# The last norms of a fused eight-block network on one core: from channel-major sums by matmul to token-major statistics

## The chip, the core and the metric

The kernel runs on one core of one Trainium2 chip. A core has five engines that run their own instruction queues beside each other and wait for one another by semaphores: TensorE (PE, matmuls and transposes), VectorE (DVE), ScalarE (ACT), GpSimd (POOL) and SyncE (SP, which here issues DMAs). Matmuls write PSUM; everything else lives in SBUF, 128 partitions wide. The metric is device time of one launch in microseconds.

## The reference

A batch of 8 sequences of 256 tokens with 128 channels (2048 tokens) passes through eight blocks, each followed by a residual addition and a layer norm over the channels, without gain and offset:

```
x = layernorm(x + rglru(x));        x = layernorm(x + local_attention(x))
x = layernorm(x + mamba(x));        x = layernorm(x + experts1(x))
x = layernorm(x + chunked_attention(x)); x = layernorm(x + experts2(x))
x = layernorm(x + typed_attention(x));   x = layernorm(x + ternary_linear(x))

def layernorm(x): m, v = mean(x), var(x);  return (x - m) / sqrt(v + 1e-5)

experts2:  shared = silu(x @ sg) * (x @ su) @ sd          # 1024 hidden channels, every token
           routed = sum over a token's 2 chosen experts of gate * expert(x)   # 8 experts, capacity 320
           result = shared + routed
typed_attention: 16 heads of 8 channels, causal, half of the heads with a decay;
           softmax(q k^T / sqrt(8) + bias) v, then @ w_o
ternary_linear:  x @ w_eff + bias
```

The change concerns the last four lines of work: the sum and the norm behind experts2, and the two norms and the linear layer behind typed attention. What feeds them is the norm behind chunked attention.

## The kernel before, in words

The kernel is written stage by stage (`rglru`, `local_mamba`, `moe1`, `chunked`, `moe2`, `typed`), and each stage mixes several pieces of work by Python generators: a `yield` in a piece is where the mixer may go on with another one. The order in which the Python code issues instructions is, for each engine, close to the order in which it runs them.

**Layouts.** Activations between the stages are held by channel: a tile of 128 partitions (channels) by 2048 columns (tokens), `y` or `self.x`. By token means 128 tokens on the partitions and 128 channels in the row; a sequence then is two such halves, `[128, 2, 128]`.

**Two ways to norm.** `layernorm_steps` (L426) works by channel. The mean over the partitions is a matmul with a constant matrix (`ln_mean`), then DVE subtracts, ACT squares, a second matmul sums the squares (`ln_var`), ACT computes the inverse root as `Exp(-0.5 * Ln(v + eps))`, and DVE multiplies. All of it runs over 128x256 per sequence. `normed` (L1240), used in the chunked stage, works by token: `bn_stats` and `bn_aggr` on DVE give mean and variance of each row, ACT computes the inverse root for 128x2 numbers, and one DVE `tensor_scalar` per half subtracts and scales. `by_channel` (L1256) then transposes the result on PE.

**The end of `chunked`** (L1399). Each sequence's normed rows `z` are transposed into `y`, and `route2` makes the routing from them.

**`moe2`** (L1470). The common expert runs in four pieces of 512 tokens, `shared(i)` (L1486): 8 steps of two matmuls (`pg`, `pu`), a Silu on ACT, a product `sh` on DVE, and one matmul that adds to `acc` (128 channels by 512 tokens). Piece 0 comes ahead of the routed experts, piece 1 behind the issue of the gathers, pieces 2 and 3 after that. `got` (L1542) holds, for each of 16 token groups, two gathered rows per token, fetched by POOL's indirect DMA. `results(b)` (L1544) multiplies them by the gates, adds them, transposes the sum (`back`), adds the common expert's piece, norms by `layernorm_steps` and leaves the result in `y`. `results(0)` and the projections of sequence 0 are advanced one step after each step of pieces 2 and 3. ACT's function table has to be changed between Silu and Ln/Exp; `exp_ln` (L414) asks for the second, and `self.norm` and `self.silu` keep some of these in order.

**`typed`** (L1722). A sequence is six units: two of the first 128 queries (8 heads each) and four of the second (4 heads each, 256 keys). The loop over units is a pipeline of four: for unit i it issues the transposes `pt` of unit i-3, the scores `sc` of unit i, the softmax of unit i-1 and the outputs `o` of unit i-3. The softmax is: the row maximum `nm` on DVE (L1681), eight or four exponentials with row sums on ACT (L1686), the reciprocal `rc` on DVE (L1688), and the product `e * rc` on POOL (L1689, 128x1024). Between these, one to three steps of `side` work are issued: `results(b+2)`, the projections `before(b+2)`, and `after(b)` (L1726), which is the output projection `wo` with its residual and norm, the ternary layer `lin` with its bias, residual and norm, and the DMA out. So the order on each engine is set by this loop: a step of `side` stands behind the softmax instructions of the unit that was issued ahead of it. All matmuls, whichever piece calls them, are recorded at L394, and transposes of `pt` at L475.

Of the kernel before, what the change touches and what calls it, by code (L numbers as in the profile page):

```python
# [12 lines left out]
F32 = mybir.dt.float32  # L13
BF = mybir.dt.bfloat16
I32 = mybir.dt.int32
AF = mybir.ActivationFunctionType
ALU = mybir.AluOpType
# [4 lines left out]
P = 128  # L22
B = 8
S = 256
T = B * S
NT = T // P
EPS = 1e-5
# [127 lines left out]
def _layout(d):  # L155

    d = {k: np.asarray(v) for k, v in d.items()}
    f = np.float32
    out = {}
# [59 lines left out]
    for l in range(2):  # L219
        w = d["L0_ffn_wqkv"][l]  # L220
        q, k, v = w[:, :512], w[:, 512:1024], w[:, 1024:]
# [15 lines left out]
    rows = np.zeros((96, 4, P), f)  # L237
    rows[::32] = np.stack([d["L2_attn_" + n] for n in ("la_pb", "lf_b2", "sa_pb", "pf_b2")])
    out["b2"] = rows.reshape(96, 4 * P)
    out["w2"], out["wf"] = np.concatenate(lay, 1), np.concatenate(ffn, 1)  # L240
    for n in ("rg", "ru", "rd", "sg", "su", "sd"):
        out["e2" + n] = d["L2_ffn_" + n]
# [54 lines left out]
class _Kernel:  # L297
# [128 lines left out]
    def layernorm_steps(self, pool, src, dst, eps=EPS, tag="ln", steps=False):  # L426

        nc = self.nc
        n = src.shape[-1]
        if not steps and n <= S:  # L430

            ps = self.psum(name="ln")
            xc, var = ps[:, 0:n], ps[:, S : S + n]
            self.mm(xc, self.centre, src)
            sq = pool.tile([P, n], F32, tag=tag + "sq", name="ln_sq", bufs=2)
            nc.scalar.activation(sq, xc, AF.Square)
            self.mm(var, self.mean, sq)
            rs = pool.tile([P, n], F32, tag=tag + "rs", name="ln_rs", bufs=2)
            nc.scalar.activation(rs, var, AF.Ln, bias=eps)
            nc.scalar.activation(rs, rs, AF.Exp, scale=-0.5)  # L440
            nc.vector.tensor_mul(dst, xc, rs)
            return
        mean = self.psum(name="ln_mean")[:, :n]
        self.mm(mean, self.mean, src)
        xc = pool.tile([P, n], F32, tag=tag + "xc", name="ln_xc")
        nc.vector.tensor_sub(xc, src, mean)
        sq = pool.tile([P, n], F32, tag=tag + "sq", name="ln_sq")
        nc.scalar.activation(sq, xc, AF.Square)
        yield
        var = self.psum(name="ln_var")[:, :n]  # L450
        self.mm(var, self.mean, sq)
        rs = pool.tile([P, n], F32, tag=tag + "rs", name="ln_rs")
        nc.scalar.activation(rs, var, AF.Ln, bias=eps)
        self.norm = nc.scalar.activation(rs, rs, AF.Exp, scale=-0.5)
        yield
        nc.vector.tensor_mul(dst, xc, rs)  # L456

    def softmax(self, small, work, sc, groups, keys, tag):

# [888 lines left out]
    def chunked(self):  # L1348
        nc, tc = self.nc, self.tc
        w = self.wf  # L1350
        y = self.y_next
# [4 lines left out]
        with (  # L1356
# [42 lines left out]
            def one_sequence(b):  # L1399
# [33 lines left out]
                nc.any.tensor_copy(y[:, cs], self.by_channel(z))  # L1433
                yield 0.3, 0.8
                self.logits(b, y, self.w1[:, 866:874], self.lg2[:, 2 * b : 2 * b + 2, :])
                assert self.routed == b
                self.routed = b + 1
                self.rest = self.route2(b, z, work, small)
# [5 lines left out]
                    next(self.rest)  # L1444

            self.routed = 0
            on_pe([one_sequence(b) for b in range(B)], 3, [self.typed_weights(prep)])
        self.chunk_scope.close()
        self.x = y
# [20 lines left out]
    def moe2(self):  # L1470
# [9 lines left out]
        with (  # L1480
# [5 lines left out]
            def shared(i):  # L1486
                cs = bass.ts(i, 512)
                acc = self.psum("S", "acc")
                for c in range(8):
                    pg, pu = self.psum("A", "pg"), self.psum("A", "pu")  # L1490
                    self.mm(pg, gu[:, 0, c * P : (c + 1) * P], x[:, cs])
                    self.mm(pu, gu[:, 1, c * P : (c + 1) * P], x[:, cs])
                    h = work.tile([P, 512], F32, tag="sh", name="sh")
                    i = nc.scalar.activation(h, pg, AF.Silu)
                    if self.norm:

                        self.issue_after([i], self.norm)
                        self.norm = None
                    self.silu = i
                    self.paced = nc.vector.tensor_mul(h, h, pu)  # L1500
                    self.mm(acc, down[:, c * P : (c + 1) * P], h, c == 0, c == 7)
                    yield
                s = keep.tile([P, 512], F32, name=f"s{i}")
                nc.vector.tensor_add(s, acc, x[:, cs])
                ss.append(s)


            self.norm = None
# [34 lines left out]

            def results(b, work):  # L1544

                ps = self.psum("M", "back")
                for j in range(2):
                    t = 2 * b + j
                    r1, r2 = got[t]

                    i = nc.vector.tensor_scalar(r1, r1, self.gate2[:, 0, t : t + 1], None, ALU.mult)
                    self.issue_after([i], self.paced)
                    nc.vector.scalar_tensor_tensor(r1, r2, self.gate2[:, 1, t : t + 1], r1, ALU.mult, ALU.add)  # L1553
                    nc.tensor.transpose(ps[:, j * P : (j + 1) * P], r1, self.ident)
                s = work.tile([P, S], F32, tag="s", name="s")
                nc.vector.tensor_add(s, ss[b // 2][:, b % 2 * S : (b % 2 + 1) * S], ps[:, 0:S])
                yield
                if b == 0:
                    self.exp_ln(self.silu)
                yield from self.layernorm_steps(work, s, y[:, bass.ts(b, S)], steps=True)  # L1560

            self.results = results
            for _ in shared(1):
                pass
            self.x = y
# [145 lines left out]
    def typed_start(self):  # L1711
        one, self.ty, self.tys = self.pool("ty1"), self.pool("ty", 2), self.pool("tys", 6)
        self.vms, self.inputs = [], {}
        for i in range(2):
            vm = one.tile([P, 2, 8 * 136], F32, name=f"vm{i}")
            self.nc.gpsimd.memset(vm, 0.0)
            self.vms.append(vm)

    def typed_before(self, b):
        self.inputs[b] = yield from self.typed_inputs(self.x[:, bass.ts(b, S)], self.vms[b % 2], self.ty)  # L1720

    def typed(self):  # L1722
# [3 lines left out]
        def after(b, o):  # L1726
            cs = bass.ts(b, S)
            ot = work.tile([P, S], F32, tag="ot", name="ot")
            nc.scalar.copy(ot, o)
            yield  # L1730
            ps = self.psum("M", "wo")
            self.mm(ps[:, 0:S], self.w3[:, 640:768], ot)
            s = work.tile([P, S], F32, tag="s", name="s")
            nc.vector.tensor_add(s, ps[:, 0:S], self.x[:, cs])
            yield
            yield from self.layernorm_steps(work, s, s, steps=True)
            ps = self.psum("M", "lin")
            self.mm(ps[:, 0:S], we, s)
            s2 = work.tile([P, S], F32, tag="s2", name="s2")
            nc.vector.scalar_tensor_tensor(s2, ps[:, 0:S], self.v("bias"), s, ALU.add, ALU.add)  # L1740
            yield
            yield from self.layernorm_steps(work, s2, s2, steps=True)
            nc.sync.dma_start(self.out[:, cs], s2)

        units = [(b, u) for b in range(B) for u in [(0, 0, 4), (0, 4, 8)] + [(1, r, r + 2) for r in range(0, 8, 2)]]
        n = len(units)
# [70 lines left out]
```

## Time and profile before

| | |
|---|---|
| runs | 1905.53, 1902.89, 1902.8 us; median 1902.89 |
| the profiled execution's own time | 1898.62 us |
| its span | 1896.8 us |
| granted TensorE clock, mean | 0.91 |
| PE / DVE / ACT / POOL busy | 84% / 58% / 54% / 30% |
| moe2 after the gathers to the end | 1578 to 1897 us |
| steady state of typed | about 1680 to 1840 us, one sequence each 31.7 us |

In the profile a line gives engine, source line, operation, the tile written and read with their shapes, and a time; `x2` counts instructions that were put together. The line of stretches gives, from left to right, the window and its length, busy time of PE, PE's weight loads, DVE, ACT and POOL with their counts, the granted clock (1.00 is full), the busy share of the DMA engines and GB/s. In the timeline, brackets at the end of a line hold the idle time of that engine ahead of the instruction and what ended it.

### The profile page before, as it was taken

The numbers are of one execution on the slowest core, as the hardware profiler recorded it, in microseconds if no ns is written. First come the engines' busy times: TensorE is split into PE (matmuls) and PEld (weight loads), VectorE is DVE, ScalarE is ACT, GpSimd is POOL, SyncE is SP. The second block draws the span as 40 slices with busy tenths as digits, with TensorE's granted clock in tenths as the row PEclk, the third lists the DMA queues.
The fourth block names the chain that finished last, engine by engine and source line by source line (L and its number), as shares of the span: only waits on it lengthen the run. The fifth ranks groups of instructions, "written<-read, shape, count | busy, mean of one in ns | idle before, by whom it ended". The sixth has DMA issues, their size and how long they took to land. (4 is left out here: it accounts for less than half of the span.)

```text
span 1896.8 us, 28424 instructions
## 1 busy us (share of the span) xinstructions
PE 1585.0 (84%) x10810; PEld 957.3 (50%) x10810; DVE 1093.2 (58%) x2011; ACT 1020.7 (54%) x2702; POOL 560.4 (30%) x493
## 2 busy tenths in 40 slices
PE   3678887878788778786679999999988987899997
PEld 2344554535454444343656566665554733455554
DVE  5734458687779686679234554456443222467664
ACT  4557777667767877554234455444433312365654
POOL 1324443344342423203120211111111042255452
PEclk7789998989899988888789999999998997899998
DMA  4000002111112122366300000000101310000000
GB/s 172 1 1 1 1 35 56 35 56 35 45 46 56 35 56 68 95 215 167 102 24 2 10 6 6 6 5 5 36 2 29 104 39 13 1 4 4 7 4 9
DMA packets 58328, 75.50 MB, mean 40 GB/s; under 512 B 5868, under 2 KB 35236, under 8 KB 57168
## 3 DMA queue, kind: packets, MB, share of 16 engines
q1 hardware_dynamic: 52864, 67.57, 12.2%
q0 software_dynamic: 3216, 5.07, 0.9%
q8 instruction: 85, 1.39, 0.3%
q10 hardware_dynamic: 2112, 1.05, 0.2%
q14 instruction: 51, 0.42, 0.1%
HBM read 65.46 MB, written 9.71 MB: 40 GB/s over the span
## 5 line engine op out<-in xcount | busy, mean ns | idle before, releaser
L394 PE MATMUL y<-hs,ident 128*128 128x512 f32 x256 | 152.7, 727 | 38.0 <-DVE hs L794 37.8
L793 DVE TENSOR_TENSOR_SCAN hs<-da,hs 128x1024 f32<-128x1024 f32 x64 | 153.5, 2404 | 1.8 <-ACT da L789 1.6
L475 PE MATMUL pt<-ident,e 128*128 128x128 f32 x768 | 125.6, 291 | 23.7 <-POOL e L652 12.4
L652 POOL TENSOR_TENSOR e<-e,rc 128x1024 f32<-128x1024 f32 x32 | 67.9, 2121 | 232.6 <-DVE rc L651 232.6
L1686 ACT ACTIVATE e<-sc,nm 128x128 f32<-128x128 f32 (+1 forms) x256 | 104.1, 424 | 59.8 <-DVE nm L1681 57.5
L789 ACT ACTIVATE da<-d,na 128x255 f32<-128x255 f32 x256 | 111.8, 503 | 37.6 <-DVE hs L793 18.8
L1689 POOL TENSOR_TENSOR e<-e,rc 128x1024 f32<-128x1024 f32 x48 | 91.9, 1915 | 135.7 <-DVE rc L1688 102.4
L647 ACT ACTIVATE e<-sc,nm,rn 128x128 f32<-128x128 f32 x256 | 113.4, 462 | 24.9 <-DVE nm L642 22.4
L475 PEld LDWEIGHTS pt<-ident,e 128*128 128x128 f32 x768 | 90.2, 147 | 64.1 <-issue 22.4
L1298 POOL TENSOR_TENSOR e<-e,rc 128x512 f32<-128x512 f32 x32 | 33.5, 1048 | 295.7 <-DVE rc L1297 178.9
L599 POOL TENSOR_TENSOR t<-t,t 128x512 f32<-128x512 f32 x64 | 90.9, 1421 | 95.4 <-DVE t L586 79.0
L477 ACT COPY ptsb<-pt 128x512 f32<-128x512 f32 x94 | 55.1, 587 | 96.3 <-PE pt L475 87.5
L791 DVE TENSOR_TENSOR hs<-u,bc 128x1024 f32<-128x1024 f32 x64 | 86.2, 1357 | 34.0 <-POOL u L778 29.4
L394 PEld LDWEIGHTS y<-hs,ident 128*128 128x128 f32 x256 | 53.8, 226 | 97.6 <-DVE hs L794 51.7
L1273 ACT COPY kp<-kps 128x512 f32<-128x512 f32 x128 | 74.8, 584 | 41.7 <-PE kps L394 39.8
L1122 POOL DMA_INDIRECT got<-ybuf,get x48 | 45.5, 949 | 162.2 <-DMA ybuf<-ys 116.7
L477 DVE COPY ptsb<-pt 128x512 f32<-128x512 f32 x98 | 65.6, 685 | 33.5 <-PE pt L475 33.3
L394 PE MATMUL qk<-w_local,h 128*128 128x512 f32 x128 | 71.5, 648 | 14.1 <-DVE t L586 9.7
L794 DVE TENSOR_TENSOR hs<-hs,bc 128x1024 f32<-128x1024 f32 x64 | 80.0, 1256 | 0.2
L1246 DVE BATCH_NORM_STATS2 st<-out 128x6 f32<-128x128 f32 x80 | 20.0, 288 | 93.8 <-PE out L394 86.8
L1681 DVE TENSOR_REDUCE nm<-sc 128x4 f32<-128x1024 f32 (+1 forms) x48 | 58.6, 1220 | 24.6 <-PE sc L394 24.3
L1309 ACT COPY vs<-vps 128x512 f32<-128x512 f32 x64 | 37.4, 584 | 65.6 <-PE vps L394 44.1
(394 smaller groups left out, 3899.9 us busy)
## 6 DMA issues: line engine op xcount, KB each, us to landing
bc<-xs SPq DMA_DIRECT2D x128, 256.0 KB
w_attn<-in_w_dram SPq DMA_DIRECT2D x4, 1024.0 KB
w_local<-in_w_dram SPq DMA_DIRECT2D x2, 1557.0 KB
places<-zeros SPq DMA_DIRECT2D x2, 1280.0 KB
w_moe<-in_e1gate_dram SPq DMA_DIRECT2D x8, 256.0 KB
w_moe<-in_e1up_dram SPq DMA_DIRECT2D x8, 256.0 KB
w_moe<-in_e1down_dram SPq DMA_DIRECT2D x8, 256.0 KB
w_moe<-in_e2rg_dram SPq DMA_DIRECT2D x8, 256.0 KB
```

Source lines behind the costliest of these rows:

```text
L394: return self.nc.tensor.matmul(out, lhsT, rhs, start=start, stop=stop)
L475: self.last = self.nc.tensor.transpose(pt[:, j * P : (j + 1) * P], src[:, j * P : (j + 1) * P], self.ident)
L477: self.nc.any.tensor_copy(sb.rearrange("p a b -> p (a b)"), pt)
L599: nc.gpsimd.tensor_add(t1, t1, t2)
L647: nc.scalar.activation(e[:, j, g, :], scs[:, j, g, :], AF.Exp, bias=nm[:, j, g : g + 1], scale=rq[:, j, g : g + 1], accum_out=sm[:, j, g : ...
L789: nc.scalar.activation(da[:, n, c, 1:S], d[:, c, 1:S], AF.Exp, scale=na[:, i : i + 1])
L791: nc.vector.tensor_tensor(hs, u.unsqueeze(1).to_broadcast(shp), bn, ALU.mult)
L793: nc.vector.tensor_tensor_scan(line(hs), line(da), line(hs), 0.0, ALU.mult, ALU.add)
L794: nc.vector.tensor_tensor(hs, hs, cn, ALU.mult)
L1273: nc.scalar.copy(k[:, 2 * i : 2 * i + 2, :].rearrange("p a b -> p (a b)"), ps)
L1686: nc.scalar.activation(e[:, i, :], sc[:, i, :], AF.Exp, bias=nm[:, i : i + 1], accum_out=sm[:, i : i + 1])
L1689: nc.gpsimd.tensor_tensor(e, e, rc.unsqueeze(2).to_broadcast([P, n, keys]), ALU.mult)
```

## The change

After it, the sums and norms behind experts2 and typed attention are by token.

- `chunked` also stores each sequence's rows `z` in a DRAM buffer, by token (128 KB on SP's queue).
- `shared(i)` loads 512 tokens of these rows into `s{i}` (256 KB) and computes `acc` by token: four matmuls of 128 columns with the hidden tile stationary in the place of one of 512. The sum goes into the loaded tile.
- `results(b)` adds the four gated rows straight into that tile with `scalar_tensor_tensor`, norms with the new `token_norm`, and transposes the normed rows into `y` with the new `channels`. The tile is kept, as `self.rows(b)`.
- `after(b)` computes `wo` and `lin` by token (two matmuls of 128 columns each, activations stationary), takes the residual from `self.rows(b)`, norms with `token_norm`, transposes once for `lin` and once for the output, and adds the bias on POOL, from a tile `bias3` in which `typed_start` loads the bias row into all partitions. The copy out of PSUM is on ACT in both places, and the DMA out takes that copy.

The diff, without the bias row's place in the inputs:

```diff
@@ -454,6 +455,28 @@
         self.norm = nc.scalar.activation(rs, rs, AF.Exp, scale=-0.5)
         yield
         nc.vector.tensor_mul(dst, xc, rs)
+
+    def token_norm(self, src, dst, small):
+
+        nc = self.nc
+        st = small.tile([P, 2, 6], F32, tag="st", name="st")
+        mv = small.tile([P, 2, 2], F32, tag="mv", name="mv")
+        for t in range(2):
+            nc.vector.bn_stats(st[:, t, :], src[:, t, :])
+            nc.vector.bn_aggr(mv[:, t, :], st[:, t, :])
+        rs = small.tile([P, 2], F32, tag="rs", name="rs")
+        nc.scalar.activation(rs, mv[:, :, 1], AF.Ln, bias=EPS)
+        self.norm = nc.scalar.activation(rs, rs, AF.Exp, scale=-0.5)
+        yield
+        for t in range(2):
+            nc.vector.tensor_scalar(dst[:, t, :], src[:, t, :], mv[:, t, 0:1], rs[:, t : t + 1], ALU.subtract, ALU.mult)
+
+    def channels(self, z, dst, copy):
+
+        ps = self.psum("M", "zt")
+        for t in range(2):
+            self.nc.tensor.transpose(ps[:, t * P : (t + 1) * P], z[:, t, :], self.ident)
+        copy(dst, ps[:, 0:S])
 
     def softmax(self, small, work, sc, groups, keys, tag):
 
@@ -1433,6 +1456,7 @@
                 nc.any.tensor_copy(y[:, cs], self.by_channel(z))
                 yield 0.3, 0.8
                 self.logits(b, y, self.w1[:, 866:874], self.lg2[:, 2 * b : 2 * b + 2, :])
+                nc.sync.dma_start(self.zrows[b * S : (b + 1) * S, :].rearrange("(t p) d -> p t d", p=P), z)
                 assert self.routed == b
                 self.routed = b + 1
                 self.rest = self.route2(b, z, work, small)
@@ -1444,6 +1468,7 @@
                     next(self.rest)
 
             self.routed = 0
+            self.zrows = self.dram.tile([T, P], F32, name="rows_chunked")
             on_pe([one_sequence(b) for b in range(B)], 3, [self.typed_weights(prep)])
         self.chunk_scope.close()
         self.x = y
@@ -1486,23 +1511,26 @@
             def shared(i):
                 cs = bass.ts(i, 512)
                 acc = self.psum("S", "acc")
+                s = keep.tile([P, 4, P], F32, name=f"s{i}")
+                nc.sync.dma_start(s, self.zrows[512 * i : 512 * (i + 1), :].rearrange("(t p) d -> p t d", p=P))
+                ss.append(s)
                 for c in range(8):
                     pg, pu = self.psum("A", "pg"), self.psum("A", "pu")
                     self.mm(pg, gu[:, 0, c * P : (c + 1) * P], x[:, cs])
                     self.mm(pu, gu[:, 1, c * P : (c + 1) * P], x[:, cs])
                     h = work.tile([P, 512], F32, tag="sh", name="sh")
-                    i = nc.scalar.activation(h, pg, AF.Silu)
+                    self.silu = nc.scalar.activation(h, pg, AF.Silu)
                     if self.norm:
 
-                        self.issue_after([i], self.norm)
+                        self.issue_after([self.silu], self.norm)
                         self.norm = None
-                    self.silu = i
                     self.paced = nc.vector.tensor_mul(h, h, pu)
-                    self.mm(acc, down[:, c * P : (c + 1) * P], h, c == 0, c == 7)
+                    for t in range(4):
+                        ts = slice(t * P, (t + 1) * P)
+                        self.mm(acc[:, ts], h[:, ts], down[:, c * P : (c + 1) * P], c == 0 and t == 0, c == 7 and t == 3)
                     yield
-                s = keep.tile([P, 512], F32, name=f"s{i}")
-                nc.vector.tensor_add(s, acc, x[:, cs])
-                ss.append(s)
+                s = s.rearrange("p t d -> p (t d)")
+                nc.vector.tensor_add(s, acc, s)
 
 
             self.norm = None
@@ -1543,23 +1571,22 @@
 
             def results(b, work):
 
-                ps = self.psum("M", "back")
+                z = self.rows(b)
                 for j in range(2):
                     t = 2 * b + j
-                    r1, r2 = got[t]
-
-                    i = nc.vector.tensor_scalar(r1, r1, self.gate2[:, 0, t : t + 1], None, ALU.mult)
-                    self.issue_after([i], self.paced)
-                    nc.vector.scalar_tensor_tensor(r1, r2, self.gate2[:, 1, t : t + 1], r1, ALU.mult, ALU.add)
-                    nc.tensor.transpose(ps[:, j * P : (j + 1) * P], r1, self.ident)
-                s = work.tile([P, S], F32, tag="s", name="s")
-                nc.vector.tensor_add(s, ss[b // 2][:, b % 2 * S : (b % 2 + 1) * S], ps[:, 0:S])
+                    for k in range(2):
+
+                        i = nc.vector.scalar_tensor_tensor(z[:, j, :], got[t][k], self.gate2[:, k, t : t + 1], z[:, j, :], ALU.mult, ALU.add)
+                        if k == 0:
+                            self.issue_after([i], self.paced)
                 yield
                 if b == 0:
                     self.exp_ln(self.silu)
-                yield from self.layernorm_steps(work, s, y[:, bass.ts(b, S)], steps=True)
+                yield from self.token_norm(z, z, self.tys)
+                self.channels(z, y[:, bass.ts(b, S)], nc.vector.tensor_copy)
 
             self.results = results
+            self.rows = lambda b: ss[b // 2][:, b % 2 * 2 : b % 2 * 2 + 2, :]
             for _ in shared(1):
                 pass
             self.x = y
@@ -1715,6 +1742,8 @@
             vm = one.tile([P, 2, 8 * 136], F32, name=f"vm{i}")
             self.nc.gpsimd.memset(vm, 0.0)
             self.vms.append(vm)
+        self.bias3 = one.tile([P, P], F32, name="bias3")
+        self.nc.sync.dma_start(self.bias3, self.ins["rows"].to_broadcast([P, P]))
 
     def typed_before(self, b):
         self.inputs[b] = yield from self.typed_inputs(self.x[:, bass.ts(b, S)], self.vms[b % 2], self.ty)
@@ -1728,19 +1757,31 @@
             ot = work.tile([P, S], F32, tag="ot", name="ot")
             nc.scalar.copy(ot, o)
             yield
-            ps = self.psum("M", "wo")
-            self.mm(ps[:, 0:S], self.w3[:, 640:768], ot)
-            s = work.tile([P, S], F32, tag="s", name="s")
-            nc.vector.tensor_add(s, ps[:, 0:S], self.x[:, cs])
+            ps = self.psum("M", "wo")[:, 0:S]
+            for t in range(2):
+                ts = slice(t * P, (t + 1) * P)
+                self.mm(ps[:, ts], ot[:, ts], self.w3[:, 640:768], t == 0, t == 1)
+            s = work.tile([P, 2, P], F32, tag="s", name="s")
+            flat = lambda a: a.rearrange("p t d -> p (t d)")
+            nc.vector.tensor_add(flat(s), ps, flat(self.rows(b)))
             yield
-            yield from self.layernorm_steps(work, s, s, steps=True)
-            ps = self.psum("M", "lin")
-            self.mm(ps[:, 0:S], we, s)
-            s2 = work.tile([P, S], F32, tag="s2", name="s2")
-            nc.vector.scalar_tensor_tensor(s2, ps[:, 0:S], self.v("bias"), s, ALU.add, ALU.add)
+            yield from self.token_norm(s, s, small)
+            st = work.tile([P, S], F32, tag="st", name="s_t")
+            self.channels(s, st, nc.scalar.copy)
+            nc.gpsimd.tensor_tensor(s, s, self.bias3.unsqueeze(1).to_broadcast([P, 2, P]), ALU.add)
             yield
-            yield from self.layernorm_steps(work, s2, s2, steps=True)
-            nc.sync.dma_start(self.out[:, cs], s2)
+            ps = self.psum("M", "lin")[:, 0:S]
+            for t in range(2):
+                ts = slice(t * P, (t + 1) * P)
+                self.mm(ps[:, ts], st[:, ts], we, t == 0, t == 1)
+            s2 = work.tile([P, 2, P], F32, tag="s2", name="s2")
+            nc.vector.tensor_add(flat(s2), ps, flat(s))
+            yield
+            yield from self.token_norm(s2, s2, small)
+            s3 = work.tile([P, S], F32, tag="s3", name="s3")
+            self.channels(s2, s3, nc.scalar.copy)
+            yield
+            nc.sync.dma_start(self.out[:, cs], s3)
 
         units = [(b, u) for b in range(B) for u in [(0, 0, 4), (0, 4, 8)] + [(1, r, r + 2) for r in range(0, 8, 2)]]
         n = len(units)
```

## The prediction

> **What bounds the kernel now.** I read the page's totals first, then the stretches, the chain, and last the timeline at each place that the change touches. TensorE (PE) is busy 84% of the span, and in the slices of the last stages nearly always. Each digit is the busy tenth of 47 us:
>
> ```profile
> PE 1585.0 (84%) x10810; PEld 957.3 (50%) x10810; DVE 1093.2 (58%) x2011; ACT 1020.7 (54%) x2702; POOL 560.4 (30%) x493
> PE   3678887878788778786679999999988987899997
> ```
>
> In stretches (PE, weight loads, DVE, ACT, POOL busy us, then clock) the changed part has three kinds of time:
>
> ```profile
> 1550.00:1600.00 50.00, 31.86 (x68) 13.43 (x67) 10.32 (x22) 13.00 (x17) 23.87 (x24) 0.76 0.10 28
> 1600.00:1650.00 50.00, 45.31 (x139) 19.88 (x137) 20.20 (x34) 17.03 (x60) 10.10 (x7) 0.90 0.00 0
> 1700.00:1750.00 50.00, 49.08 (x365) 30.23 (x365) 33.70 (x62) 29.14 (x118) 29.26 (x18) 1.00 0.01 4
> 1850.00:1897.00 47.00, 36.33 (x264) 21.65 (x260) 21.15 (x38) 20.48 (x82) 11.71 (x6) 0.87 0.03 9
> ```
>
> The first two (gathers, typed start) and the last (tail) are latency: PE waits and its clock falls. From about 1680 to 1840 PE is full at clock 1.00; there one sequence takes 31.7 us (wo at 1711.19 and 1742.97), so about five of the eight sequences run in this steady state. A gain in a latency place is the length of the chain saved; in the steady state it is PE work saved, less any wait of PE put in its place.
>
> **The change part by part.** Sums are made against the profiled execution, 1898.62 us (span 1896.8, so 1.8 lies around it). It is 4.3 below the median 1902.89, and differences are carried over as they are.
>
> *Costed at nothing.* Eight 128 KB row stores, four 256 KB loads and the bias broadcast on SP: its queue idles between the chunk tiles and before the gathers, and the s tiles are needed only after 8 common-expert steps of 2.83 us; without that cover a load would cost a few us once. The acc matmul as 4 x 128 columns: the routed expert's py, which has its own weights for each 128 columns, takes .87 to .89 for 8 records, acc at 512 columns .86; the weight load hides. At most +.03 x 64 = 2 us. Engine loads: in the steady sequence DVE is busy about 22 of 31.7 us and POOL 17; the change adds some 1.6 to DVE (bn_stats, copies and scalings for subtractions and multiplies), .73 to POOL (the bias addition, in place, behind the transposes that read the same rows) and takes about 1.6 from ACT; none becomes the bound by its sum.
>
> *results(0), beside the common expert.* The norm by matmul waits for ln_var between two Silus, and each change of function reloads a table on ACT: loads at 1581.18, 1583.09, 1585.67 and 1587.40, 1.28 us each. Silus stand at 1582.47 and 1588.69, 6.2 us apart, where a step takes 2.83. The instruction order after has 2 loads where there were 5. Three loads less are 3.8, and 1 us of ln matmuls goes: -4.3 (from -3.4, the gap alone, to -5).
>
> *Typed start.* The multiply of results(1) meets POOL's softmax product, and proj waits for it at clock .50:
>
> ```profile
> 1633.83 1.90 POOL L1689 TENSOR_TENSOR e<-e,rc 128x1024 f32<-128x1024 f32 x1 [38.05 <-DVE rc L1688]
> 1633.85 2.15 DVE L456 TENSOR_TENSOR x_moe<-ln_xc,ln_rs 128x256 f32<-128x256 f32 x1
> ```
>
> After, no step goes to PE and back for mean and variance (1630.2 to 1633.4 is the chain now), so the rows can be ready ahead of that POOL op: -3.5; -1 if they aren't, -5 if the clock recovers too.
>
> *Tail.* From the end of ot (1881.98) to the last multiply (1894.04) there are 12.06 us of pure chain. One link of it:
>
> ```profile
> 1890.57 0.43 DVE ln_xc L446
> 1891.00 0.02 issue
> 1891.02 0.42 ACT ln_sq L448
> 1891.44 0.04 issue
> 1891.49 1.23 PE ln_var L394 x2
> 1892.72 0.02 issue
> 1892.74 0.39 ACT ln_rs L453
> ```
>
> A matmul norm there costs 1.24 + .43 + .42 + 1.23 + .39 + .42 + .43 = 4.6 with gaps of .03. By rows: two bn_stats (.288) and two aggregates (.17) = .92, Ln and Exp on 128x2 (.205 each) = .41, two scalings (.336 by the nearest row, two-scalar TENSOR_SCALAR from SBUF to SBUF) = .67, two transposes at half clock .5, ACT copy .37: 2.9 with the gaps. Twice: -3.3.
>
> *Steady state, PE work.* For each sequence six norm passes of 256 columns go. The row for one is .70 for its two records, of which the next instruction is put off .63 (1719.81 to 1720.44); I take .6: -3.6. Two score units are split now by such a pass; sc at 1718.76 to the mask's end at 1722.21 is 3.45, less .63 = 2.8, where an unsplit one takes 1.6. After, the order has every score unit whole: 2 x -1.0. Added are two pairs of transposes, .27 each. Net -5.0 a sequence.
>
> *Steady state, new waits.* Against this stand the scalings of the rows. In DVE's order each pair follows right behind a softmax reciprocal rc, and this rc also releases POOL's product of 1.9 us. What happens to a DVE op [...] beside it:
>
> ```profile
> 1719.40 0.45 DVE L1551 TENSOR_SCALAR got<-got,gate 128x128 f32<-128x128 f32 x2
> 1719.63 1.97 POOL L1689 TENSOR_TENSOR e<-e,rc 128x1024 f32<-128x1024 f32 x1 [2.44 <-DVE rc L1688]
> 1719.77 1.98 DVE L1553 SCALAR_TENSOR_TENSOR got<-got,gate 128x128 f32<-128x128 f32 x1
> ...
> 1814.51 2.12 DVE L1551 TENSOR_SCALAR got<-got,gate 128x128 f32<-128x128 f32 x2
> 1814.60 1.95 POOL L1689 TENSOR_TENSOR e<-e,rc 128x1024 f32<-128x1024 f32 x1 [2.44 <-DVE rc L1688]
> ```
>
> The op that comes second takes 1.98 where alone it takes .34. [...] Does each pair lose the race? The reciprocal takes .17 and POOL starts .31 to .34 after its start, so DVE has .15; one scaling may slip in, the other waits until POOL is done, plus .28. If none waited, this item would be 0; [...]
> - s: with wo at 0, rc at 3.6, POOL 3.9 to 5.8, second scaling done 6.2, transposes to 6.6, ACT copy to 7.2, lin 7.25. PE, done with pt and sc at 3.9, stands 2.3 and then .4 more: 2.7.
> - s2: rc at 10.4, POOL 10.6 to 12.6; PE is done at 10.9 and gets its transposes near 12.9: 2.0.
> - The four gate products of the results [...] then end at 13.7, and queued behind them on DVE is the next score maximum nm, for which ACT's exponentials and with them POOL and the next pt wait: about 1.6 by the time they reach PE. The third scaling pair lies inside the last o steps.
>
> Together 6.3 of wait against 5.0 of work: +1.3 a sequence, +6.5 for five. Bounds: -5 (every wait filled) to +3 (the third pair and the bias addition on POOL, .73 by the row of that size, before its next product, also reach PE).
>
> *Sum.* The start of the second sequence, where both kinds overlap, +.5. -4.3 - 3.5 - 3.3 + .5 + 6.5 = -4.1: 1894.5 for the profiled execution, 1898.8 on the median.
>
> **The rivals.** Below, 0.2% (3.8 us) is what a measurement of this kernel can tell from no change.
>
> *The waits win.* If each scaling pair loses its race and the delay passes to nm, and so to the next race, the steady sequence is 3 to 4.5 longer: +15 to +22 against the gains of 10.6 elsewhere: 1907 to 1915. For it: the order has rc directly ahead of every pair. Against: PE has other work queued for part of it. It decides from +2.1 us a sequence (equal to before), and tells as slower from +2.9.
>
> *PE's work decides.* POOL's products and the scalings miss each other, as most of the 24 norm multiplies did before (mean of the s ones .425, unblocked). Then -3 to -5 a sequence: 1867 to 1883. Against: before, the multiply was behind a wait for PE, not behind rc.
>
> *Nothing to see.* Gains and waits cancel: 1899.1 to 1906.7.
>
> *The clock.* [...] the waits worked out here are at most 2.7[...]. If it drops once a sequence, [...]: +17 for five, 1916. That is the top of the range.
>
> **How the numbers follow.** My sum's own case (steady +0.5 to +2) has 0.4 and spans 1894 to 1904; its middle is on the edge of what can be told. Waits win (with the clock): 0.33. PE's work decides: 0.27. Faster by over 0.2% is the last whole and 0.15 of the first: 0.42; within 0.2%: 0.21, most of it from the first; slower: 0.37. Range with one tenth out on each side: 1878 to 1914. Predicted: 1898.8.
>
> **What would show it.** Right: in the steady state the scaling pairs appear with one near 2 us beside POOL's e, PE idle before zt is put down to them, and a period near 33; the tail from ot to the last copy near 8.8; two table loads in results(0); proj of results(1) before 1634. Wrong: scalings at .34 throughout and a period of 27 to 29 (PE's work decides), or a period over 34 and a clock under 1.00 between 1680 and 1840.

## The result: slower by 1.6%

The changed kernel takes 1932.66 us (median of 4 runs, 1928.89 to 1935.3) beside 1904.16 for the kernel before: ratio 1.0163, 95% interval 1.0149 to 1.0178. The forecast was 1898.8, with 1878 to 1914 as its range; the time lies outside. Its profiled execution took 1928.89 us, span 1927.1, so 30.3 us more span than before.

First the same view as before the change, the page's totals and PE's row of the 40 slices, then the stretches (window, length, busy time of PE, weight loads, DVE, ACT and POOL, clock, DMA share, GB/s), of the changed kernel:

```profile
PE 1571.9 (82%) x10970; PEld 975.6 (51%) x10970; DVE 1122.3 (58%) x2106; ACT 1006.6 (52%) x2692; POOL 563.7 (29%) x501
...
PE   3667878778788788776699999999879949888886
```

```profile
1550.00:1600.00 50.00, 25.52 (x93) 15.26 (x94) 9.76 (x24) 7.15 (x11) 22.45 (x24) 0.73 0.10 29
1600.00:1650.00 50.00, 45.00 (x217) 24.91 (x216) 22.66 (x43) 18.80 (x64) 11.79 (x9) 1.00 0.00 0
1650.00:1700.00 50.00, 44.46 (x334) 27.46 (x333) 36.91 (x73) 24.77 (x111) 24.98 (x16) 0.94 0.01 4
1700.00:1750.00 50.00, 42.92 (x281) 26.88 (x282) 32.25 (x63) 23.21 (x103) 20.82 (x15) 0.83 0.01 4
```

Where the typed stage was full before (49.1 of 50 at clock 1.00), PE now stands for 7 us of 50, and what it does runs at a mean clock of 0.83. The last row names the loss; the second shows that the start of the stage got better (clock 1.00 where it was 0.90).

The difference by stretches, from PE's rows of both profiled executions (first gather on POOL, last common-expert step, the eight `wo`, end of the span):

| stretch | before | after | difference | forecast |
|---|---|---|---|---|
| start to first gather | 1534.8 | 1535.8 | +1.1 | 0 |
| first gather to the last common-expert step | 90.0 | 96.5 | +6.5 | -4.3 |
| to the first wo (typed start) | 54.8 | 47.1 | -7.7 | -3.5 and +0.5 |
| first to sixth wo (five steady sequences) | 158.3 | 185.2 | +26.9 | +6.5 |
| sixth to eighth wo (drain) | 44.1 | 49.5 | +5.4 | 0 |
| eighth wo to the end (tail) | 14.8 | 13.0 | -1.8 | -3.3 |
| sum | 1896.8 | 1927.1 | +30.3 | -4.1 |

Most of it lies in the steady sequences, and there the forecast's own list of waits can be compared place by place. In the timeline of the changed kernel (start, length, instruction, idle time before it and what ended it), 3.5 us after the `wo` at 1717.54:

```profile
1721.07 0.17 DVE L1715 RECIPROCAL rc<-sm 128x4 f32<-128x4 f32 x1
...
1721.36 2.26 DVE L472 TENSOR_SCALAR s<-s,mv,rs 128x128 f32<-128x128 f32 x2
...
1721.38 1.89 POOL L1716 TENSOR_TENSOR e<-e,rc 128x1024 f32<-128x1024 f32 x1 [0.33 <-DVE rc L1715]
```

```profile
1723.51 0.50 PE L478 MATMUL zt<-ident,s 128*128 128x128 f32 x2 [1.81 <-DVE s L472]
1723.93 0.65 PE L395 MATMUL o<-ptsb,vm 128*64 128x128 f32 x6
1724.51 1.02 PE L395 MATMUL lin<-we,s_t 128*128 128x128 f32 x4
1725.46 1.54 PE L395 MATMUL o<-ptsb,vm 128*64 128x128 f32 x10
1726.94 1.67 PE L498 MATMUL pt<-ident,e 128*128 128x128 f32 x8
```

The scaling and POOL's product start within 0.02 us of one another, and the pair of scalings takes 2.26 us where it takes 0.60 in the tail, with POOL idle (at 1916.53). All 15 pairs between the first and the sixth `wo` lose in this way (2.15 to 2.29 us). PE waits 1.81 us for this one. This was forecast. What was not is the rest of the second fence: ten `o` and eight `pt` take 1.54 and 1.67 us, where the same eight `pt` take 1.09 at 1719.11. The granted clock says why. In the traces of the kernel before and of the changed one (92 and 108 stretches at one clock) every stretch but the last, which the end of the trace cuts off, is a whole number of 3.41 us long, so that all changes lie on one grid. The next rows are windows of it (PE's busy time is the number after the comma, the clock the third from the end):

```profile
1721.36:1724.77 3.41, 1.60 (x14) 1.00 (x13) 3.39 (x3) 0.37 (x1) 2.58 (x2) 1.00 0.00 0
1724.77:1728.18 3.41, 3.41 (x20) 2.85 (x20) 1.08 (x5) 1.93 (x8) 0.04 (x1) 0.50 0.00 0
1728.18:1731.59 3.41, 2.25 (x13) 0.85 (x11) 3.41 (x7) 0.41 (x2) 1.91 (x1) 1.00 0.00 0
...
1735.01:1738.42 3.41, 1.31 (x12) 0.52 (x8) 1.97 (x3) 2.06 (x13) 1.33 (x1) 1.00 0.01 3
1738.42:1741.83 3.41, 2.70 (x13) 1.60 (x14) 2.47 (x4) 0.00 (x0) 0.57 (x1) 0.50 0.00 0
1741.83:1745.24 3.41, 3.41 (x12) 2.01 (x13) 0.69 (x1) 2.48 (x13) 0.00 (x0) 0.50 0.01 2
1745.25:1748.66 3.41, 3.41 (x34) 2.58 (x30) 1.96 (x4) 2.58 (x14) 1.20 (x1) 1.00 0.00 0
```

A window in which PE was busy for 1.60 us, and one with 1.31, are each followed by half clock (0.50), for one window and for two; after the one with 2.25 us it stayed at 1.00. The five steady sequences have nine such falls, at least one each.

### The profile page after: what moved, and what is told of

Its sections match the earlier page's. It is cut to its first block, busy times and chain, and to the rows that moved or that the text cites. A ratio compares the mean times of both kernels' runs of the same rounds, so it can differ in the third digit from the quotient of the medians.

```text
span 1927.1 us, 28821 instructions
## 1 busy us (share of the span) xinstructions
PE 1571.9 (82%) x10970; PEld 975.6 (51%) x10970; DVE 1122.3 (58%) x2106; ACT 1006.6 (52%) x2692; POOL 563.7 (29%) x501
## 4 chain that ended last, share of the span: by engine, by line
PE 50%; DVE 19%; ACT 12%; issue 7%; POOL 7%; another core or an unknown queue 3%; DMA 2%; ACTq 0%; SPq 0%; POOLq 0%; DVEq 0%
PE vps L395 7%; PE kps L395 5%; PE sc L395 5%; PE pt L498 4%; PE out L395 4%; PE o L395 4%; DVE hs L816 3%; PE pu L395 3%; PE pg L395 3%; ACT e L670 3%; DVE hs L817 2%; DVE hs L814 2%; DVE s L472 2%; PE y L395 2%
## 5 line engine op out<-in xcount | busy, mean ns | idle before, releaser
L498 PE MATMUL pt<-ident,e 128*128 128x128 f32 x768 | 129.6, 303 | 26.6 <-POOL e L675 12.2
L812 ACT ACTIVATE da<-d,na 128x255 f32<-128x255 f32 x256 | 111.8, 502 | 37.7 <-DVE hs L816 18.8
L498 PEld LDWEIGHTS pt<-ident,e 128*128 128x128 f32 x768 | 95.4, 154 | 66.2 <-issue 23.1
L1527 DVE TENSOR_TENSOR sh<-sh,pu 128x512 f32<-128x512 f32 x32 | 22.0, 688 | 88.3 <-PE pu L395 49.8
```

The costliest lines, as they stand in the source:

```text
L498: self.last = self.nc.tensor.transpose(pt[:, j * P : (j + 1) * P], src[:, j * P : (j + 1) * P], self.ident)
L812: nc.scalar.activation(da[:, n, c, 1:S], d[:, c, 1:S], AF.Exp, scale=na[:, i : i + 1])
```

## The experiments

The theory, read from the fences above: beside POOL's product of 1.89 us a scaling that reads and writes SBUF on DVE is held up (2.26 us for the pair in the place of 0.60); since the same `rc` starts both, the loss recurs three times a sequence; PE waits, and the waits bring the clock down. Rivals: the chain of statistics, inverse root, scaling and transposes is too long wherever the scaling reads; the waits alone cost, the clock doesn't; only one of the three norms matters. The ratios below are to the kernel before in the same group of runs, for the groups lie at two levels: with the result and in the first and fourth group the kernel before takes 1900 to 1904 us, in the second and third 1846 to 1847. Some of the expectations put this down to the chip; the record numbers the chip of the first and of the second group alike (5), so that isn't shown.

**The scalings read PSUM.** The scaling stays, and so does its place behind `rc`; its source moves, and with it the result of the addition ahead of it, which the statistics read too. A line of issue order keeps the gate products behind it.

```diff
-            nc.vector.tensor_add(flat(s), ps, flat(self.rows(b)))
+            nc.vector.tensor_add(ps, ps, flat(self.rows(b)))
             yield
-            yield from self.token_norm(s, s, small)
+            yield from self.token_norm(ps.rearrange("p (t d) -> p t d", t=2), s, small)
 ...
-            nc.vector.tensor_add(flat(s2), ps, flat(s))
+            nc.vector.tensor_add(ps, ps, flat(s))
             yield
-            yield from self.token_norm(s2, s2, small)
+            yield from self.token_norm(ps.rearrange("p (t d) -> p t d", t=2), s2, small)
```

> The two scalings of the typed norms read the sum from PSUM and write SBUF; the scaling of the experts' results stays SBUF to SBUF. Same instructions, same place behind rc. Theory [...]: one of the new scalings takes 0.40 us, PE's waits of 1.8 and 1.2 us ahead of zt go, the wait of 2.8 us for the results stays; a steady sequence falls from 37.7 to about 33 us, the time to about 1910. Rival (the chain itself is too long, [...]): scalings are short but PE still waits at zt; time within 5 us of 1932.7.

Measured: 1890.37 us, ratio 0.9947 (0.9930 to 0.9965). Faster than both kernels, by more than was expected. The groups by form of this run (count, busy time, mean ns) hold the blocked scaling of the results' rows and, beside it, the two that read PSUM:

```profile
L472 DVE TENSOR_SCALAR s<-s,mv,rs 128x128 f32<-128x128 f32 x16 | 13.9, 906 | 1.6 <-ACT rs L469 1.0
L472 DVE TENSOR_SCALAR s<-wo,mv,rs 128x128 f32<-128x128 f32 x16 | 5.8, 405 | 1.7 <-ACT rs L469 1.0
L472 DVE TENSOR_SCALAR s<-lin,mv,rs 128x128 f32<-128x128 f32 x16 | 5.8, 406 | 4.0 <-ACT rs L469 4.0
```

And at the place that was shown above, in its timeline:

```profile
1714.47 0.73 DVE L472 TENSOR_SCALAR s<-wo,mv,rs 128x128 f32<-128x128 f32 x2
...
1714.50 1.89 POOL L1718 TENSOR_TENSOR e<-e,rc 128x1024 f32<-128x1024 f32 x1 [0.34 <-DVE rc L1717]
```

Both run at once: 0.73 us for the pair under a product of 1.89, where the pair from SBUF took 2.26. So here the source of the scaling decides, and the rival of the long chain falls: PE's waits ahead of `lin` and of the second transposes are gone with the same instructions on another memory. The line of issue order came with it and was not tried alone, but that one scaling takes 405 ns beside a product of 1.89 us is read from the instruction itself and doesn't hang on the order.

**All three scalings on ACT.**

```diff
-            nc.vector.tensor_scalar(dst[:, t, :], src[:, t, :], mv[:, t, 0:1], rs[:, t : t + 1], ALU.subtract, ALU.mult)
+            nc.scalar.activation(nb[:, t, 0:1], nb[:, 2, t : t + 1], AF.Identity, scale=rs[:, t : t + 1])   # nb[:, 2] = -mean
+            nc.scalar.activation(dst[:, t, :], src[:, t, :], AF.Identity, bias=nb[:, t, 0:1], scale=rs[:, t : t + 1])
```

> All three scalings go to ACT (Identity with scale and bias, and three small ACT instructions for the bias). Theory [...]: none can be blocked by POOL; PE's waits at zt fall from 5.8 us a sequence to under 2, clock near 1.00, steady sequence 28 to 31 us, time 1885 to 1900, below the kernel before. Rival (chain too long): the 1.3 us more on ACT delay exponentials, time 1925 or more.

Measured: 1888.31 us, ratio 0.9939 (0.9916 to 0.9961); steady sequence 30.1 us, clock 1.00. One sequence each, of the kernel before, the changed one and this one:

```profile
1711.20:1743.00 31.80, 30.93 (x225) 18.58 (x224) 22.11 (x40) 18.55 (x77) 16.59 (x11) 1.00 0.02 5
```

```profile
1717.50:1755.30 37.80, 31.95 (x221) 20.33 (x220) 25.79 (x52) 17.12 (x76) 17.26 (x12) 0.86 0.02 5
```

```profile
1709.80:1739.90 30.10, 27.82 (x221) 17.43 (x220) 21.50 (x47) 20.32 (x90) 17.27 (x12) 1.00 0.02 6
```

These three rows take the changed sequence apart. It has the 221 matmul records of this run, which are 27.8 us of PE at full clock, 3.1 below the kernel before: that is the work saved. The other 10.0 are 5.85 of PE idle (37.80 - 31.95) and 4.1 of the same work, for a part of the time at half clock (31.95 - 27.82).

**PE kept busy during the wait.** Four matmuls whose result nobody reads go ahead of each pair of transposes:

```diff
         ps = self.psum("M", "zt")
+        for _ in range(4):
+            self.mm(ps[:, S : 2 * S], self.mean, self.w3[:, 0:S])
```

> Four matmuls of 256 columns that nobody reads (1.7 us at full clock) are put ahead of each pair of zt transposes, where PE waits. Theory (the clock): about half of the 6 us a sequence are half-clock work after the waits; PE stays busy, the clock is near 1.00, steady sequence about 33 us, time about 1910, faster than the changed kernel although it does more. Rival (the waits alone): the clock is not what costs; time 1932 or more.

Measured: 1917.27 us, ratio 1.0077 (1.0057 to 1.0097). That is slower than expected (about 1910), but with 4.2 us more of PE work a sequence (32.02 against 27.82) it beats the changed kernel, as the clock's theory says; two of its five steady sequences:

```profile
1721.30:1754.70 33.40, 32.02 (x245) 21.99 (x243) 22.59 (x50) 18.06 (x78) 17.27 (x12) 1.00 0.02 5
1754.70:1789.50 34.80, 33.42 (x245) 23.00 (x244) 22.77 (x50) 18.07 (x78) 17.29 (x12) 0.95 0.02 5
```

It isn't a clean test of the clock, for the order on DVE moved with it: of the three pairs of scalings one takes 2.26 us as before, one 0.59 and one 1.73. A cleaner one was in the first experiment already. Its first two steady sequences have the same instructions and the same wait of 1.91 us of PE, for the results' rows (before the transposes at 1699.23 and 1728.35); once the clock holds and once it falls:

```profile
1681.20:1710.70 29.50, 27.14 (x221) 17.20 (x220) 22.88 (x51) 17.57 (x77) 17.29 (x12) 1.00 0.02 6
1710.70:1741.30 30.60, 28.54 (x221) 17.46 (x220) 22.91 (x51) 17.57 (x77) 17.18 (x12) 0.94 0.02 6
```

The fall costs 1.1 us of the sequence, and no other number of the two rows differs by as much, but for the busy time of PE itself. What differs is where the wait lies on the grid: once over two windows, with PE busy 2.90 and 2.00 us of 3.41, once within one:

```profile
1697.82:1701.23 3.41, 2.00 (x11) 0.85 (x11) 3.24 (x6) 2.17 (x13) 1.27 (x1) 1.00 0.00 0
1725.13:1728.54 3.41, 1.50 (x17) 1.09 (x13) 3.01 (x5) 3.38 (x22) 1.89 (x1) 1.00 0.01 2
1728.54:1731.95 3.41, 3.41 (x13) 1.13 (x14) 1.78 (x6) 0.58 (x4) 1.50 (x1) 0.50 0.00 0
```

**Typed attention by channel, the results by token.** The function `after` is that of the kernel before; the rest is as changed.

> The function behind typed attention is that of before (by channel, norms by matmul); the common expert and the experts' results are by token as in the change. Theory: one blocked scaling and the blocked gate products a sequence remain, so about a third of the loss: 1908 to 1915. Rival (the results' part is harmless, all of the loss is in the two typed norms): 1895 to 1902.

Measured: 1891.13 us, ratio 0.9938 (0.9915 to 0.9960); and once more in the third group, beside the changed kernel:

> The kernel with typed attention's norms by channel and the experts' results by token once more, on the same chip as e_psum_act, to tell which of the two is the better: steady sequence 29.1 us, tail 14.5 us, 12 to 17 us below the kernel before.

1832.12 us, ratio 0.9917 (0.9889 to 0.9944). The theory's number for it (1908 to 1915) is missed, and so is the rival's, to the fast side. Its steady sequence is 29.1 us at clock 1.00: the by-token half of the results is not a third of the loss but a gain of 2.6 us a sequence. Its scaling isn't blocked there (410 ns in the mean, PE waits nowhere longer than 0.6), while in the PSUM version it still is (2.19 us for the pair, PE waits 1.91). So what stands around this scaling decides whether it meets POOL's product.

**Only the results' scaling on ACT**, the two typed ones as changed, is the counterpart:

> Only the scaling of the experts' results goes to ACT; the two typed scalings stay SBUF to SBUF on DVE. Theory: PE's waits of 1.8 and 1.2 us remain, the third (2.8) shrinks to the 1.5 of the ACT form, one fall of the clock of two remains: steady sequence 33 to 35 us. Rival (only the results' scaling matters): 31 or less.

Measured in one run: 1852.95 us beside 1847.21 for the kernel before; steady sequences 33.2, 31.7, 33.2, 31.8 and 33.3 us. PE's waits are 1.8, 1.2 to 1.3 and 1.3. So two blocked norms cost some 2 to 4 us against the versions with none; all three blocked cost 5 to 9. The expectation of 33 to 35 holds for three of the five. They are the first, third and fifth, and in these alone the clock falls, as the first two show:

```profile
1624.55:1657.77 33.22, 28.85 (x221) 18.79 (x219) 24.22 (x51) 17.79 (x80) 17.28 (x12) 0.95 0.02 5
1657.77:1689.51 31.74, 27.28 (x220) 17.48 (x219) 24.15 (x51) 17.79 (x80) 17.28 (x12) 1.00 0.02 6
```

The same wait of 1.81 us lies within one window of the grid in the third sequence (PE busy 1.60 of 3.41 us) and over two in the fourth (2.96 and 2.05). Of the two shown, the one with the fall takes 1.5 us more (33.22 against 31.74).

**The results' transposes one step later** (a `yield` between the scaling and `channels` in `results`, on top of the PSUM form):

> As e_psum, and the transposes of the results' rows are issued one step of the unit loop later, behind more work of PE. Theory [...]: the blocked scaling of the results (2 us) is now covered by PE's o and pt, the last wait of 1.9 us a sequence and the clock's fall behind it go; steady sequence 28 to 29 us, time 1879 to 1884. Rival (the blocked scaling delays the next score maximum on DVE, and that is the cost): steady sequence 30 or more, time within 3 us of 1890.

Measured: 1833.4 us, ratio 0.9926 (0.9902 to 0.9951), steady sequences 29.1 and then 30.7 four times. The rival was right on the period: the scheduler still put the transposes where PE waits 1.91 us for them, and the clock still fell.

**No scaling beside POOL's product, the typed ones on DVE** (typed from PSUM, results on ACT):

> The typed scalings read PSUM (as e_psum) and the results' scaling is on ACT (as in e_res_act), so that no scaling can meet POOL's product. Theory: PE's only wait over 0.6 us is the 1.3 us of the ACT form, which left the clock at 1.00; steady sequence 28.5 to 29.5 us; ratio to the kernel before on the same chip 0.988 to 0.992. Rival (PE work and chain now bound it at 30): 0.993 to 0.995.

Measured: 1889.55 us, ratio 0.9938 (0.9916 to 0.9961), steady sequence 29.3 four times at clock 1.00, with one wait of 0.95, and 32.5 in the fifth, where the clock fell for 6.8 us after the same wait. The period is the theory's in four of five. The ratio missed its bracket by 0.2% and lies in the rival's; the gather stretch, told next, takes 5.7 us (95.7 against 90.0) and the fifth sequence 3.2. Beside the 29.1 of the version with typed attention by channel, the 29.3 also says that the typed half by token saves nothing in the steady sequence, even unblocked; what it gains lies behind it (sixth to eighth `wo` 41.5 us against 44.1, tail 13.5 against 14.5). The five versions that beat the kernel before lie at 0.992 to 0.995, and their intervals overlap; none is shown to be the best.

**The stretch under the gathers.** In the profiles at the level of 1900 us DVE stands still in the middle of the common expert while POOL issues its gathers. In the changed kernel:

```profile
1552.95 0.69 DVE L1527 TENSOR_TENSOR sh<-sh,pu 128x512 f32<-128x512 f32 x1 [7.17 <-remote]
1578.29 0.69 DVE L1527 TENSOR_TENSOR sh<-sh,pu 128x512 f32<-128x512 f32 x1 [24.65 <-remote]
```

and in the kernel before, later and in more pieces:

```profile
1560.79 0.69 DVE L1504 TENSOR_TENSOR FunctionType.Silu _12055<-acc,x_chunked 128x512 f32<-128x512 f32 x1 [6.31 <-remote]
1564.30 0.69 DVE L1500 TENSOR_TENSOR sh<-sh,pu 128x512 f32<-128x512 f32 x1 [2.83 <-remote]
1578.22 0.42 DVE L1556 TENSOR_TENSOR s<-FunctionType.Silu _11529,back 128x256 f32<-128x256 f32 x1 [12.31 <-remote]
```

At this level it is 19.8 us from the first gather to the eighth common-expert step before, and 45.7 to 48.5 in all versions by token. Three runs asked what part of the change does this. The first is the kernel before with only the form of acc changed:

```diff
-                    self.mm(acc, down[:, c * P : (c + 1) * P], h, c == 0, c == 7)
+                    for t in range(4):
+                        ts = slice(t * P, (t + 1) * P)
+                        self.mm(acc[:, ts], h[:, ts], down[:, c * P : (c + 1) * P], c == 0 and t == 0, c == 7 and t == 3)
```

> The kernel before with one edit: acc as four matmuls of 128 columns with the hidden tile stationary (its sum then has tokens where the rest takes channels, so this leaves out the common expert's proper sum). Question: from the first gather to the end of the eighth common-expert step the kernel before takes 20 us and every kernel by token 46 to 48. If the form of acc is the cause: 40 us or more. If it is what stands around it (order, loads, chance): 25 or less. In the undisturbed steps: 2.87 us in place of 2.83.

> The kernel before once more, for its gather stretch: if the 20 us from the first gather to the end of the eighth common-expert step are its own, they come again within 5 us; if they are chance, they are nearer to the 46 of the kernels by token.

> The changed kernel once more, beside the two below on one chip. On the first chip DVE stood still for longer while POOL issued the gathers (last common-expert step 96 us after the first gather, 90 before); without that stretch the loss is that of the steady sequences: if the gather stretch is as before here, 24 to 28 us slower than the kernel before; if it isn't, 28 to 34.

All three fell at the level of 1847 us. There the eighth step comes 18.9 us (form of acc), 18.6 (before) and 18.6 (changed) after the first gather, and DVE shows no such wait in any of them. The changed kernel takes 1873.43 us there, ratio 1.0158 (1.0131 to 1.0184), its steady sequences 35.5, 37.7, 37.7, 35.1 and 36.6: the loss is the same without the gather stretch. So these stops come with the level and not with the change alone. The form of acc costs 0.7 us over the 24 steps (68.7 against 68.0, one run each). What DVE waits for in the stops (the profile puts them down to `remote`, and names no engine or DMA), and why the versions by token meet it two steps earlier, is open.

## Why the prediction was wrong

**The waits of the steady sequence: the race right, the sum in part by luck.** Forecast 2.7 + 2.0 + 1.6 = 6.3; in the sequence shown they are 1.81, 1.22 and 2.81, 5.84 in all, and every pair of scalings lost its race (2.26, 2.15 and 2.19 us). That POOL's product would hold up the new scaling too was carried over from the gate products of the trace of before, where one SCALAR_TENSOR_TENSOR took 1.98 us (0.34 in the median) and one TENSOR_SCALAR from SBUF to SBUF, at 1814.71, 1.92 (0.28); it held in all 15 pairs. But the first two were taken too long, and the third is another wait than the one forecast: the 1.6 was for a delayed score maximum, while PE stood 2.81 us for the third scaling pair itself, which the prediction put inside the last `o` steps and kept only for its upper bound.

**PE's saving: too large.** The step that took 31.7 - 5.0 = 26.7 us for a sequence's PE work; it is 27.8. The work saved is 3.1 (30.93 to 27.82) and not 5.0; 0.9 of the sequence before was already idle.

**The clock: this step failed.** The sum left the clock at 1.00 through waits of at most 2.7 us, which the trace of before didn't show: its PE has no such wait in the steady sequences. The fall was left to a rival, and its price of 17 us was the author's estimate. In the changed kernel waits of 1.8 to 2.8 us were followed by half clock in every steady sequence, at a cost of 4.1 us in the one shown. 33.0 was forecast and 37.7 came: 4.1 is the clock, 1.1 the work, less 0.5 on the waits. In the steady sequences of its trace nine windows of the grid at full clock had PE busy for 0.96 to 1.61 us of 3.41, and each of the nine was followed by half clock; of the 33 others at full clock, with 1.71 us and up, none was. In the steady sequences of before all 47 windows had 2.61 us and up, and none was. So what told the falls apart here is not the length of a wait but how much of it, with the idle time beside it, fell into one window. The longest wait of the list shows it: in the fourth sequence of the changed kernel its 2.81 us lie over two windows, with PE busy for 1.71 and 2.30 us, and the clock holds.

```profile
1814.62 0.33 PE L478 MATMUL zt<-ident,s 128*128 128x128 f32 x1 [2.81 <-DVE s L472]
```

```profile
1810.10:1813.51 3.41, 1.71 (x14) 0.52 (x8) 1.97 (x5) 2.46 (x15) 0.93 (x1) 1.00 0.00 0
1813.51:1816.92 3.41, 2.30 (x20) 1.72 (x20) 2.77 (x4) 0.14 (x1) 0.97 (x1) 1.00 0.01 2
```

It isn't the whole of it: in the version with no scaling beside POOL's product the clock fell in the fifth sequence after a wait of 0.95 us, with PE busy for some 2.5 of the 3.41 us ahead of the slowed matmuls. What brought it down there is open.

**The drain: costed at 0 by being left out.** The seventh and eighth sequences have no results to make, but the two typed norms, and lost 5.4 us together.

**results(0): the right mechanism, the wrong size, and hidden.** Two table loads stand where there were five (one at 1571.13 and the four that were listed):

```profile
1587.98 1.28 ACT L417 ACT_TABLE_LOAD   x1
1589.28 0.20 ACT L468 ACTIVATE rs<-mv 128x2 f32<-128x2 f32 x1
1589.51 0.20 ACT L469 ACTIVATE rs<-rs 128x2 f32<-128x2 f32 x1
1589.73 1.28 ACT L1522 ACT_TABLE_LOAD   x1
```

The Silus around them are 3.7 us apart and no longer 6.2. But the term of -4.3 (whose parts, 3.8 and 1, add up to 4.8) took all of that gap as lost time, though PE filled part of it with the projections (1.96 us), and a step with acc in four pieces takes 2.87 in place of 2.83. At the level without the stops the whole stretch gained 1.5 us (68.0 to 66.5).

**Typed start and tail: right in kind, off in size.** Forecast -3.0 and -3.3. The start gained 7.7 in the first profiles and 3.7 at the other level (52.0 to 48.3), with proj 5.5 and 6.7 us after the last common-expert step where it was 11.3. The chain from wo to the last copy fell from 12.0 to 7.9, a little more than forecast, but 2.3 of it are given back between that copy and the end of the span, where no engine's instruction is recorded, so the tail gained 1.8.

**The way it ended.** The rivals "waits win" and "the clock" together name what happened; the first was priced at +3 to +4.5 a sequence and the second at +17 for all five. Measured: +5.4 a sequence, +26.9. The clock's 1916 was called the top of the range, which ends at 1914; the two rivals together, which is what came, lie outside it. (The rival "PE's work decides" ends at 1877 by its own terms, 1902.9 - 10.6 - 15, and not at 1883; nothing hangs on that.)

## What to carry to other kernels

When an instruction is moved from one operand memory to another, ask which engine starts on the same event: here an SBUF-to-SBUF scaling behind the reciprocal that also releases a GpSimd product lost the race in all 15 pairs (2.15 to 2.29 us a pair, 0.60 without the product), and a scaling that read the same sum from PSUM took 0.41 us, against 0.34 for one from SBUF that nothing held up, and removed the wait. Price a wait of TensorE not at its length alone: in a stage that is full, add the slowed work behind it, here 1.1 to 1.6 us for each fall of one window of 3.41 us and 4.1 in a sequence with three such windows. Whether the wait of 1.81 us brought a fall here depended on whether it lay within one window (PE busy 1.60 of 3.41 us) or over two (2.96 and 2.05), so two sequences with the same waits differed by some 1.5 us. And take such a change apart before judging it: the results by token alone were good for 0.6 to 0.8%, and the place of two operands in the typed half is the difference between a loss of 1.6% and a gain of 0.5%.

## What was not expected of the hardware

In the traces of the kernel before and of the changed one the granted clock changed only on a grid of 3.41 us. In the steady sequences of the changed kernel each of the nine windows at full clock with TensorE busy for 1.61 us or less was followed by half clock in the next one or two; full work on both sides (3.41 us in the windows from 1717.94 and from 1724.77) didn't prevent it. A wait of 1.91 us (scalings from PSUM) or of 1.81 us (results' scaling on ACT) was followed by half clock in one sequence and not in the one beside it, and a wait of 2.81 us in the changed kernel left it at 1.00. And the same kernel took 1900 us in some groups of runs and 1847 in others; in the profiles 28 of that lie ahead of the first gather (1534.8 against 1506.9) and 22 under and after the gathers (90.0 against 68.0), while the steady sequences agree to 0.1 us. What sets the level is open.
